# A residual added by accumulating transfers from memory instead of by VectorE

## Chip, core and metric

The kernel runs on one core of a Trainium2 chip. The metric is the device time of one execution in microseconds (us), the median of several runs. Five engines work side by side, each through its own queue in order: TensorE (PE; its weight loads are shown apart as PEld), VectorE (DVE), ScalarE (ACT), GpSimd (POOL) and SyncE (SP), which here only issues transfers. A tile in on-chip memory has 128 partitions; PSUM is the small memory that TensorE writes.

## What is computed

Multi-query attention with a residual, over 64 batches of 128 tokens with 512 features, 16 heads of width 64, one key and one value head shared by all of them:

```python
xn = layernorm(x, g_in)
q  = (xn @ Wq).reshape(b, n, H, DH).transpose(0, 2, 1, 3) * scale
kv = xn @ Wkv                      # k, v, each with one null row ahead
sim = einsum('bhid,bjd->bhij', q, k) + bias     # causal and key masks
out = einsum('bhij,bjd->bhid', softmax(sim), v) # -> (b, n, 1024)
return x + layernorm(out @ Wo, g_out)
```

All is float32. The change concerns the last line: `layernorm(out @ Wo, g_out)` of batch `b` is held in a tile `y_b` of 128 x 512, and `x[b]`, 256 KB in memory, is added to it before the store.

## The kernel before

The work goes in 32 steps of two batches each, called pairs; `body(d)` (L1311) is one step of a software pipeline, written out by hand, and `turn(d)` (L1024) is the short piece ahead of it. Every engine runs its instructions in the order in which these functions name them. In step `d` four pairs are under way: `a, b = 2d, 2d + 1` are in the scores and softmax, `p, p + 1 = 2d - 2, 2d - 1` in the output product, `l, l + 1 = 2d - 4, 2d - 3` in the output norm, the residual and the store, and batches of a coming group of four (`g`) have their input normed, transposed and projected. The residual is done in this way in steps 2 to 29, for 56 batches; the last two steps and the tail have code of their own, which the change leaves alone.

A step is even or odd (`h = d % 2`). They differ in two places that matter here:

- In an **odd** step up to 27, SP sends the normed and transposed tokens of the next group to memory and back: `tokens_out` (L333, tile `xd`, 1024 KB out) and `tokens_in` (L339, tile `xT`, four transfers of 256 KB in), where the latter wait for the former.
- In an **even** step, GpSimd has more to do: `token_sum` (L485), `token_sums_inner` (L556) and, from step 4 to 28, `token_sums_last` (L617), whose four subtractions write `xM` and `xS` for the matmuls `pm` of `last_product` (L633).

GpSimd also does `out_sum` (L904, four sums of tile `oT` for the output product), `scale` (L769, the softmax's factor onto the scores `s`) and `bias_add` (L676). VectorE's `blocks_T` (L783) transposes the scaled scores; behind it in VectorE's queue stands `out_keep("X", "yu2", ...)` (L945, L948), which copies the PSUM tile `pyX` to `kyu` before product 7 is added to `pyX`.

The output side of a pair: `out_product` (L918) makes seven products in PSUM tiles `pyX`, `pyY` and `pyw`; `out_part` (L952, the addition at L966) writes halves of `y_b`. For batch `p + 1` it reads `pyX` near the step's end, and the last product, number 4, may be added to `pyX` only after that. Tiles `y` come from a pool of three buffers, so `y` of `p + 1` gets the buffer of `y` of `l = p - 2`, and its first `out_part` waits until the store of `l` has read it. In the next step `pair_stats` and `pair_pow` make the norm's numbers, `pair_norm` (L990, ScalarE) writes the normed rows to a PSUM tile `yn`, `pair_gain` (L996) multiplies `yn` in place by the gain `gob`, `pair_residual` (L999) adds `res` and writes `y`, and `store` (L1002, on SP) sends it out. `load_res` (L126) loads `res` for the step after, at the end of SP's part of the step.

Of the kernel before, what the change touches and what calls it, by code (L numbers as in the profile page):

```python
# [11 lines left out]
ALU = mybir.AluOpType  # L12
# [5 lines left out]
def kernel(  # L18
# [59 lines left out]
    nc = tc.nc  # L78
# [34 lines left out]
    xs, res, m8s = {}, {}, {}  # L113
# [12 lines left out]
    def load_res(b):  # L126
        pool, tag = (rp, "res")
        if b >= B - 5:
            pool, tag = (gp, "xT") if b == B - 1 else (xp, "x")
        res[b] = pool.tile([P, DIM], FP, tag=tag, name=f"res_{b}")  # L130
        nc.sync.dma_start(out=res[b], in_=x[b])
# [20 lines left out]
    gob = const.tile([P, DIM], FP, name="gob")  # L152
# [186 lines left out]
    def tokens_in(g):  # L339
        xT[g] = gp.tile([P, GB, KC, N], FP, tag="xT", name=f"xT_{g}")  # L340
        xd = xds.pop(g).rearrange("(i p) j e -> j p i e", p=Q)
        for j in range(NQ):
            nc.sync.dma_start(
                out=xT[g][j * Q : (j + 1) * Q].rearrange("p i c n -> p i (c n)"),
                in_=xd[j],
            )
# [152 lines left out]
    def product(g, f, k, pool, tag, start=True):  # L499

        if start:
            prod[tag] = pool.tile([P, HT], FP, tag=tag, name=f"p{tag}_{g}_{f}_{k}")
        lo, hi = xT[g][:, 0 : GB // 2], xT[g][:, GB // 2 :]
        t1, t2, t3, t4 = (xS.get((g, i)) for i in range(1, 5))
        w, t = {
            1: (a11, lo[:, :, lo_k]),
            2: (a12, lo[:, :, hi_k]),
            3: (s4, hi[:, :, hi_k]),
            4: (a22, t4),
            5: (s1, t1),  # L510
            6: (s2, t2),
            7: (s3, t3),
        }[k]
        for kc in range(HK):
            nc.tensor.matmul(  # L515
                prod[tag],
                w[:, kc, f * P : (f + 1) * P],
                t[:, :, kc, :],
                start=(start and kc == 0),
                stop=(kc == HK - 1),  # L520
                skip_group_check=not start,
            )

    def keep(tag, name, slot=None):
        slot = slot or name
        kept[name] = bp.tile([P, HT], FP, tag=f"k{slot}", name=f"k{name}", bufs=1)
        nc.scalar.copy(kept[name], prod[tag])  # L527
# [251 lines left out]
    oT, ys = {}, {}  # L779
# [124 lines left out]
    def out_sum(p, k, eng=nc.gpsimd):  # L904

        h11, h12 = oT[p][:, 0], oT[p][:, 1]
        h21, h22 = oT[p + 1][:, 0], oT[p + 1][:, 1]
        if k == 0:
            yS[p] = bp.tile([P, HC, N], FP, tag="yS", name=f"yS_{p}", bufs=1)
        o, a, b, op = (  # L910
            (yS[p], h21, h22, ALU.add),
            (h11, yS[p], h11, ALU.subtract),
            (h21, h22, h11, ALU.subtract),
            (h12, h12, h11, ALU.subtract),
        )[k]
        eng.tensor_tensor(o, a, b, op)  # L916

    def out_product(p, k, pool, tag, start=True):  # L918
        key = "y" + tag
        if start and pool is ps_s:  # L920
            two = ps_s.tile([P, 2, DIM], FP, tag="s", name=f"py_{p}_{k}_s")
            prod[key] = two[:, 0, 0:HE]
        elif start:
            prod[key] = pool.tile([P, HE], FP, tag=tag, name=f"py{tag}_{p}_{k}")
        a, b = oT[p], oT[p + 1]
        h, w = {
            1: (a[:, 0], e11),
            2: (a[:, 1], e21),
            3: (a[:, 1], e22),
            4: (b[:, 1], sums_e[3]),  # L930
            5: (yS.get(p), sums_e[0]),
            6: (a[:, 0], sums_e[1]),
            7: (b[:, 0], sums_e[2]),
        }[k]
        for c in range(HC):
            nc.tensor.matmul(  # L936
                prod[key],
                h[:, c, :],
                w[:, c, :],
                start=(start and c == 0),  # L940
                stop=(c == HC - 1),
                skip_group_check=not start,
            )

    def out_keep(tag, name, slot):  # L945
        kept[name] = bp.tile([P, HE], FP, tag=f"k{slot}", name=f"k{name}", bufs=1)
        if name == "yu2":
            nc.vector.tensor_copy(kept[name], prod["y" + tag])  # L948
        else:
            nc.scalar.copy(kept[name], prod["y" + tag])  # L950
# [17 lines left out]
    yn = {}  # L968
# [25 lines left out]
        nc.scalar.activation(yn[b], ys[b], AF.Identity, bias=nmr, scale=rstd)  # L994

    def pair_gain(b):  # L996
        nc.vector.tensor_tensor(yn[b], yn[b], gob, ALU.mult)

    def pair_residual(b):  # L999
        nc.vector.tensor_tensor(ys[b], yn.pop(b), res.pop(b), ALU.add)  # L1000

    def store(b):  # L1002
        nc.sync.dma_start(out=out[b], in_=ys.pop(b))
# [17 lines left out]
    PAIRS = B // 2  # L1021
# [289 lines left out]
    def body(d):  # L1311

        a, b, p, l = 2 * d, 2 * d + 1, 2 * d - 2, 2 * d - 4
        g, h = d // 2 + 1, d % 2
        q, soft = g < NG, d > 0
        out, ln = 0 <= p <= P_LAST, 0 <= l <= P_LAST
# [48 lines left out]
            norm_nmr(m + 1)  # L1365
        if ln:
            pair_gain(l)
            pair_residual(l)
            store(l)
        if soft:  # L1370
            exps(b, 0, 0, 3)
        if out:
# [3 lines left out]
        if out:  # L1376
            out_product(p, 1, ps_y, "X")
            out_keep("X", "yp1", "yp1")
            out_sum(p, 1)
            out_sum(p, 2)  # L1380
        if q:
            product(g, f0, 6, ps_q, "a", start=False)
            keep("a", "u2")
# [14 lines left out]
        if ln:  # L1398
            pair_gain(l + 1)
# [16 lines left out]
            product(g, f1, 2, ps_w, "w")  # L1416
        if ln:
            pair_residual(l + 1)
            store(l + 1)
        if xw:  # L1420
            norm_apply(m + 1)
        if soft:
# [11 lines left out]
        if xw:  # L1434
            tokens_T(m + 1)
            if h == 1:
                tokens_out(g + 1)
                tokens_in(g + 1)
        if 0 <= p:
            for r in (p, p + 1):  # L1440
                load_res(r)
        nm = m + 2
# [236 lines left out]
    for d in range(1, PAIRS - 2):  # L1679
        turn(d)  # L1680
        body(d)
# [42 lines left out]
```

## Time and profile before

| | |
|---|---|
| runs | 1022.8, 1024.07 and 1023.01 us, median 1023.01 |
| profiled execution | span 1021.2 us; this span is the execution's own time, and the runs' median is 1.8 us above it |
| busy share of the span | PE 99%, PEld 88%, DVE 83%, POOL 75%, ACT 66% |
| granted TensorE clock | 0.999 of full speed |
| transfers | 100.86 MB, mean 99 GB/s, 98.47 MB of them on SP's queue; none issued by GpSimd |

The profile's page gives for each group of instructions its line, engine, operation, tiles, shape and count, then busy time, the mean duration and the idle time ahead of them with what ended it. The timeline lists instructions in order of time, with the idle time ahead in brackets. A step of two batches takes about 31.1 us.

### The profile page before, as it was taken

To read this page: it belongs to the slowest core of one execution; us is meant where nothing else is said; L and a number is where in the kernel's file an instruction comes from. 1 tells how busy PE (TensorE), PEld (TensorE's weight loads), DVE (VectorE), ACT (ScalarE), POOL (GpSimd) and SP (SyncE) were. 2 spreads that over 40 slices of the span, in tenths; PEclk is the share of its full clock that TensorE was granted. 3 is DMA by queue.
4 is the path that set the end of the run, shared out by engine and by line. 5 is a ranking of instruction groups with operands and counts; after the bars stand their busy time and mean duration, and the time that the engine had idled before them with its cause. 6 is when DMAs were issued, how large, how long until landed. Compare 5 with 4: busy or idle time off the path is not lost.

```text
span 1021.2 us, 31459 instructions
## 1 busy us (share of the span) xinstructions
PE 1012.8 (99%) x12333; PEld 899.6 (88%) x12333; DVE 845.8 (83%) x1958; ACT 673.1 (66%) x2753; POOL 769.2 (75%) x633
## 2 busy tenths in 40 slices
PE   9999999999999999999999999999999999999997
PEld 8888888888888888888888888888888888888886
DVE  6777888888888888888888888888898888977787
ACT  5766677656677665686656776566775657865583
POOL 4997768677686877859678696776868768686686
PEclk9999999999999999999999999999999999999999
DMA  7415143151531415225152341514315152140221
GB/s 219 139 30 151 67 122 112 36 154 63 144 98 69 123 56 152 88 74 140 36 152 85 109 120 32 164 63 138 102 50 134 64 152 89 71 111 24 69 85 62
DMA packets 73835, 100.86 MB, mean 99 GB/s; under 512 B 32212, under 2 KB 36056, under 8 KB 71896
## 3 DMA queue, kind: packets, MB, share of 16 engines
q1 hardware_dynamic: 73392, 98.47, 32.5%
q8 instruction: 96, 1.57, 0.6%
q14 instruction: 51, 0.42, 0.1%
q10 hardware_dynamic: 296, 0.40, 0.1%
HBM read 63.19 MB, written 33.55 MB: 95 GB/s over the span
## 4 chain that ended last, share of the span: by engine, by line
PE 96%; POOL 1%; DVE 1%; ACT 1%; issue 0%; DMA 0%; POOLq 0%; DVEq 0%; ACTq 0%
PE pyX L936 20%; PE pa L515 16%; PE pyY L936 10%; PE pc L515 10%; PE po L849 8%; PE pkv L363 6%; PE pyw L936 5%; PE pl L581 4%; PE pm L647 4%; PE ps L718 3%; PE pq L450 3%; PE sc_X L718 2%; PE sc_Y L718 2%; PE sc_a L718 1%; PE py_s L936 1%; ACT s L749 1%
## 5 line engine op out<-in xcount | busy, mean ns | idle before, releaser
L749 ACT ACTIVATE s<-s,nmax 128x65 f32<-128x65 f32 (+1 forms) x1024 | 372.2, 369 | 61.7 <-DVE nmax L740 61.7
L771 POOL TENSOR_TENSOR s<-s,rinv 128x512 f32<-128x512 f32 (+1 forms) x132 | 190.6, 1446 | 133.1 <-DVE rinv L767 133.1
L683 POOL TENSOR_TENSOR s<-biasp,mneg 128x1552 f32<-128x1552 f32 (+1 forms) x65 | 206.2, 3176 | 50.9 <-DVE s L733 26.9
L749 ACT ACTIVATION_READ_ACCUMULATOR s<-s,nmax 128x1 f32 x1024 | 197.1, 192 | 0.0
L787 DVE STREAM_TRANSPOSE sb<-s 128x1536 f32<-128x1536 f32 (+1 forms) x68 | 113.6, 1674 | 11.4 <-POOL s L771 11.4
L740 DVE TENSOR_REDUCE nmax<-s 128x8 f32<-128x1032 f32 (+1 forms) x128 | 121.8, 952 | 0.1
L964 ACT COPY y<-pyX 128x256 f32<-128x256 f32 x29 | 10.8, 372 | 167.5 <-PE pyX L936 129.7
L936 PE MATMUL pyX<-wT,oT 128*128 128x256 f32 x464 | 109.7, 379 | 0.0
L936 PE MATMUL pyX<-wo,oT 128*128 128x256 f32 x464 | 109.7, 379 | 0.0
L936 PEld LDWEIGHTS pyX<-wo,oT 128*128 128x128 f32 x464 | 86.0, 190 | 10.5
L936 PEld LDWEIGHTS pyX<-wT,oT 128*128 128x128 f32 x464 | 84.0, 190 | 9.2
L916 POOL TENSOR_TENSOR oT<-oT 128x512 f32<-128x512 f32 x64 | 80.6, 1277 | 3.9 <-PE pyw L936 1.6
L849 PE MATMUL po<-sb,vr 32*64 32x128 f32 (+1 forms) x3904 | 82.9, 308 | 0.2 <-DVE sb L787 0.2
L527 ACT COPY ku<-pa 128x256 f32<-128x256 f32 x118 | 43.4, 367 | 59.8 <-issue 30.8
L849 PEld LDWEIGHTS po<-sb,vr 32*64 32x64 f32 x3904 | 71.7, 130 | 9.4 <-issue 5.6
L536 DVE TENSOR_TENSOR qT<-pc,ku 128x256 f32<-128x256 f32 x118 | 48.2, 408 | 32.2 <-PE pc L515 19.7
L868 ACT ACTIVATE oT<-po,nv 128x512 f32<-128x512 f32 (+1 forms) x127 | 73.5, 655 | 0.4 <-PE po L849 0.2
L515 PE MATMUL pa<-xS,wq 128*128 128x256 f32 x264 | 67.8, 379 | 0.0
L597 DVE TENSOR_TENSOR qT<-pl,kp 128x128 f32<-128x128 f32 x112 | 32.1, 286 | 42.8 <-PE pl L581 41.9
L281 POOL TENSOR_TENSOR rstd<-rstd,nhalf 128x1 f32<-128x1 f32 x64 | 35.2, 557 | 42.0 <-DVE rstd L280 38.9
L363 PE MATMUL pkv<-xT,wkv 128*128 128x256 f32 x256 | 63.3, 391 | 0.0
L515 PE MATMUL pa<-xT,wq 128*128 128x256 f32 x236 | 60.6, 379 | 0.0
(207 smaller groups left out, 2588.9 us busy)
## 6 DMA issues: line engine op xcount, KB each, us to landing
res<-in_x_dram SPq DMA_DIRECT2D x64, 256.0 KB
out_dram<-y SPq DMA_DIRECT2D x63, 256.0 KB
x<-in_x_dram SPq DMA_DIRECT2D x62, 256.0 KB
xd<-xb SPq DMA_DIRECT2D x14, 1024.0 KB
xT<-xd SPq DMA_DIRECT2D x56, 256.0 KB
vr<-vd SPq DMA_DIRECT2D x64, 128.0 KB
kT<-kT SPq DMA_DIRECT2D x32, 64.0 KB
vd<-vb SPq DMA_DIRECT2D x32, 64.0 KB
```

The source lines that it names most:

```text
L363: nc.tensor.matmul(pkv, wkv[:, kc, :], xT[g][:, t : t + 2, kc, :], start=(kc == 0), stop=(kc == KC - 1),)
L515: nc.tensor.matmul(prod[tag], w[:, kc, f * P : (f + 1) * P], t[:, :, kc, :], start=(start and kc == 0), stop=(kc == HK - 1), skip_group_ch ...
L683: nc.gpsimd.tensor_tensor(S[b][:, :, keys], biasp[:, :, keys], mneg[:, t, keys] .unsqueeze(1) .broadcast_to([P, R8, keys.stop - keys.start ...
L718: nc.tensor.matmul(home[r][u * DH : (u + 1) * DH, f, :], qT[g, f, t // 2][rows, t % 2, hf, u], kT[rows, 0 : nk // Q, t, :], start=True, st ...
L740: nc.vector.tensor_reduce(nmax[b][:, hf], S[b][:, :, WITH_NULL[hf]], AX.X, ALU.max, negate=True)
L749: nc.scalar.activation(row, row, AF.Exp, bias=nmax[b][:, hf, k : k + 1], accum_out=rsum[b][:, hf, k : k + 1],)
L771: nc.gpsimd.tensor_tensor(sv, sv, rinvs[b, hf][:, lo:hi].unsqueeze(2).broadcast_to([P, hi - lo, sv.shape[2]]), ALU.mult,)
L787: nc.vector.transpose(sbs[b][:, :, lo:hi].rearrange("p j e q -> p e j q"), S[b][:, lo:hi, 1 : ROW - 1].rearrange("p e (j k) -> p e j k", k=Q),
L849: nc.tensor.matmul(po[s][rows, to : to + n], vr[g][quad, t, PLACE[j], :], sb[quad, slots, r * NF : (r + 1) * NF, :], start=(turn == 0), st ...
L868: nc.scalar.activation(to, src, AF.Identity, bias=nv2)
L916: eng.tensor_tensor(o, a, b, op)
L936: nc.tensor.matmul(prod[key], h[:, c, :], w[:, c, :], start=(start and c == 0), stop=(c == HC - 1), skip_group_check=not start,)
```

## The change

`pair_gain` now writes its product from `yn` to `y`. `pair_residual` becomes a transfer that GpSimd issues: it reads `x[b]` from memory and adds it onto `y_b` in place. Both stores move from their places behind the residuals to one place behind `tokens_out` and `tokens_in`. The loads of `res` in the steady steps go; step 29 still loads the two that the last steps use. The transfer of `l` is issued behind `out_sum(p, 2)` instead of the addition directly behind `pair_gain(l)`; that of `l + 1` keeps its place in the code.

```diff
     def pair_gain(b):
-        nc.vector.tensor_tensor(yn[b], yn[b], gob, ALU.mult)
+        nc.vector.tensor_tensor(ys[b], yn.pop(b), gob, ALU.mult)

     def pair_residual(b):
-        nc.vector.tensor_tensor(ys[b], yn.pop(b), res.pop(b), ALU.add)
+        nc.gpsimd.dma_start(out=ys[b], in_=x[b], accum_op=ALU.add)
...
         if ln:
             pair_gain(l)
-            pair_residual(l)
-            store(l)
...
             out_sum(p, 1)
             out_sum(p, 2)
+        if ln:
+            pair_residual(l)
...
         if ln:
             pair_residual(l + 1)
-            store(l + 1)
...
                 tokens_out(g + 1)
                 tokens_in(g + 1)
-        if 0 <= p:
+        if ln:
+            store(l)
+            store(l + 1)
+        if d == PAIRS - 3:
             for r in (p, p + 1):
                 load_res(r)
```

SP's queue in an odd step before the change; `y_3115` and `y_3237` are the two batches stored, `xd` and `xT` the tokens' way out and in, `vd` the values (the numbers are the program's and differ between the two programs):

```order
L396 DMA kT<-kT 64x4x64
L137 DMA m_5_3441<-in_mask_BxS_bk_dram 128x512
L1003 DMA out_dram<-y_3115 128x512
L1003 DMA out_dram<-y_3237 128x512
L335 DMA xd_3544<-xb_3140 128x2048
L343 DMA xT_3546<-xd_3544 32x4x512 x4
L131 DMA res_3551<-in_x_dram 128x512
L131 DMA res_3553<-in_x_dram 128x512
L122 DMA x_3555<-in_x_dram 128x1x512
L122 DMA x_3557<-in_x_dram 128x1x512
```

The same step of the changed kernel:

```order
L396 DMA kT<-kT 64x4x64
L137 DMA m_5_3417<-in_mask_BxS_bk_dram 128x512
L335 DMA xd_3518<-xb_3118 128x2048
L343 DMA xT_3520<-xd_3518 32x4x512 x4
L1003 DMA out_dram<-y_3094 128x512
L1003 DMA out_dram<-y_3213 128x512
L122 DMA x_3527<-in_x_dram 128x1x512
L122 DMA x_3529<-in_x_dram 128x1x512
```

The stores have gone from ahead of `xd` to behind `xT`, into the places of the two loads of `res`.

VectorE's queue near the end of that odd step in the changed kernel; in brackets stand the counters on which an instruction waits, DMAHW for transfers that SP issued, DMASW for those of GpSimd:

```order
L966 TENSOR_TENSOR y_3497<-pyY_5_3563,kyu_3596 128x256 [waits PE_49]
L972 BN_STATS sto_3616<-y_3497 128x6 [waits DVE_49]
L974 BN_AGGR mvo_3618<-sto_3616 128x2 [waits DVE_49]
L976 TENSOR_SCALAR rstdo_3620<-mvo_3618 128x1 [waits DVE_49]
L966 TENSOR_TENSOR y_3627<-pyX_1_3460,kyp_3568 128x256 [waits DMAHW7_49,DMASW2_49,PE_49]
L536 TENSOR_TENSOR qT_3_1_3394<-pc_3_5_3570,ku_3576 128x4x64 [waits PE_49]
L663 TENSOR_TENSOR qT_3_0_3393<-pm_1_3536,ku_3603 128x2x64 [waits PE_49]
L663 TENSOR_TENSOR qT_2_0_3391<-pm_1_3536,qT_2_0_3391 128x2x64
L787 STREAM_TRANSPOSE sb_3636<-s_3195 128x8x6x32 [waits Pool_49]
```

The order is as before. `y_3627` has the buffer of `y_3094`, so the second L966 waits for the store of `y_3094`, which before stood ahead of `xd` and now stands behind `xT`.

GpSimd's queue in an even step before, from the sums of the output product to the scaling of the scores' second half:

```order
L916 TENSOR_TENSOR oT_2160<-yS_2239,oT_2160 128x512
L916 TENSOR_TENSOR oT_2160<-oT_2160 128x512 x2
L771 TENSOR_TENSOR s_1963<-s_1963,rinv_0_2266 128x8x64
L627 TENSOR_TENSOR xM_2283<-xS_3_2241 128x128
L627 TENSOR_TENSOR xS_3_2241<-xS_3_2241 128x128
L627 TENSOR_TENSOR xM_2283<-xS_3_2241,xM_2283 128x128 x2
L771 TENSOR_TENSOR s_1733<-s_1733,rinv_1_2332 128x8x128
```

The same stretch in the changed kernel:

```order
L916 TENSOR_TENSOR oT_2148<-yS_2225,oT_2148 128x512
L916 TENSOR_TENSOR oT_2148<-oT_2148 128x512
L1000 DMA y_1847<-in_x_dram 128x512
L916 TENSOR_TENSOR oT_2148<-oT_2148 128x512
L771 TENSOR_TENSOR s_1951<-s_1951,rinv_0_2253 128x8x64
L627 TENSOR_TENSOR xM_2270<-xS_3_2227 128x128
L627 TENSOR_TENSOR xS_3_2227<-xS_3_2227 128x128
L627 TENSOR_TENSOR xM_2270<-xS_3_2227,xM_2270 128x128 x2
L1000 DMA y_1972<-in_x_dram 128x512
L771 TENSOR_TENSOR s_1725<-s_1725,rinv_1_2316 128x8x128
```

Two transfers stand in GpSimd's queue that were not there, the first ahead of the last sum, the second ahead of the scaling of `s`.

## The prediction

> **What bounds the kernel now.** I read the page first: its busy shares, and the chain of work that ended last.
>
> ```profile
> PE 1012.8 (99%) x12333; PEld 899.6 (88%) x12333; DVE 845.8 (83%) x1958; ACT 673.1 (66%) x2753; POOL 769.2 (75%) x633
> PE 96%; POOL 1%; DVE 1%; ACT 1%; issue 0%; DMA 0%; POOLq 0%; DVEq 0%; ACTq 0%
> ```
>
> TensorE works through, and the chain is 96% TensorE. Then the waits: who held up TensorE at all in the steady steps.
>
> ```profile
> PEld sc_Y L718 <- issue: 10.1, 32, 0.3
> PEld pkv L363 <- DVE s L733: 4.3, 25, 0.2
> ```
>
> The largest wait of TensorE for another engine is 4.3 us in all. That is the ceiling of what freeing VectorE can bring; the issue gaps are TensorE's own. So the question is not what the change saves, but whether it makes TensorE wait.
>
> **What is taken from VectorE.**
>
> ```profile
> L1000 DVE TENSOR_TENSOR y<-yn,res 128x512 f32<-128x512 f32 x56 | 38.5, 687 | 1.0
> ```
>
> 56 additions of 687 ns, 38.5 us of VectorE's time, two per step. `pair_gain` keeps its instruction. By the row above the 38.5 us lie beside TensorE; VectorE soon waits for TensorE again in each step. I count them at nothing. The bytes read for the residual stay the same, on another queue.
>
> **Odd steps: the store behind the tokens.** The timeline of SP's queue in one odd step, and the wait ahead of `xT` over all 14 groups:
>
> ```profile
> 573.31 2.66 SPq L1003 DMA_DIRECT2D out_dram<-y  x2
> 577.44 0.33 SPq L335 DMA_DIRECT2D xd<-xb  x1
> 581.35 1.75 SPq L343 DMA_DIRECT2D xT<-xd  x4
> 583.14 0.90 SPq L131 DMA_DIRECT2D res<-in_x_dram  x2
> ...
> L343 SPq EVENT_SEMAPHORE  x14: 17/3505/4683, 80.3 to 888.6; - x14
> ```
>
> SP stands some 3.5 us (median) until `xd` has landed, then issues four `xT`. The store of `l` went out at 573.3; now it takes the place of the first `res`, at 583.14, behind 4 x 256 KB in the same queue. What waits for it is the `out_part` of `p + 1`, which reuses its buffer (the rows from VectorE's and TensorE's timelines):
>
> ```profile
> 587.06 0.42 DVE L966 TENSOR_TENSOR y<-pyX,kyp 128x256 f32<-128x256 f32 x1 [0.17 <-PE pyX L936]
> ...
> 588.77 1.77 DVE L787 STREAM_TRANSPOSE sb<-s 128x1536 f32<-128x1536 f32 x1
> ...
> 588.16 1.89 PE L936 MATMUL pyX<-wT,oT 128*128 128x256 f32 x8
> ```
>
> L966 ran at 587.06 and TensorE's product 4 at 588.16 must follow it, since it adds onto the `pyX` that L966 reads. When does the transfer in the place of the first `res` land? From the busy time by stretches (last two numbers: share of the transfer engines, GB/s):
>
> ```profile
> 582.00:583.00 1.00, 1.00 (x7) 0.87 (x6) 1.00 (x3) 0.25 (x2) 0.00 (x0) 1.00 0.42 82
> 583.00:584.00 1.00, 1.00 (x7) 0.92 (x6) 0.35 (x3) 0.37 (x1) 0.74 (x1) 1.00 0.77 256
> 584.00:585.00 1.00, 1.00 (x6) 0.87 (x6) 0.75 (x3) 0.00 (x0) 1.00 (x1) 1.00 1.04 213
> 585.00:586.00 1.00, 1.00 (x7) 0.87 (x6) 0.64 (x2) 0.00 (x0) 1.00 (x2) 1.00 1.06 219
> 586.00:587.00 1.00, 1.00 (x6) 0.90 (x5) 0.82 (x3) 0.00 (x0) 1.00 (x1) 1.00 1.06 213
> 587.00:588.00 1.00, 1.00 (x8) 0.90 (x7) 0.50 (x2) 0.00 (x0) 1.00 (x1) 1.00 1.06 211
> 588.00:589.00 1.00, 1.00 (x7) 0.92 (x7) 0.98 (x4) 0.00 (x0) 0.83 (x2) 1.00 1.00 317
> 590.00:591.00 1.00, 1.00 (x69) 1.00 (x72) 0.79 (x2) 0.37 (x1) 0.38 (x1) 1.00 0.47 116
> ```
>
> Up to 588 they add up to 1194 KB. Four `xT` and one more transfer are 5 x 262 = 1311 KB, reached at 588.4 at the earliest; the queue empties in the stretch from 590. I take 589.3 for the landing, between the two, because the slowest of 16 engines decides and later transfers share the last stretch. L966 then ends at 589.7, and with 0.1 for the signal TensorE starts product 4 at 589.8 instead of 588.16: 1.65 us lost. It is lost for good, since TensorE has no idle time to give it back; behind L966 on VectorE stand two small additions and L787, which keep their distance to TensorE.
>
> To this comes the accumulating transfer of `l + 1`. GpSimd will issue it right when `xd` is on its way out (below), and another 262 KB then share the engines. `xd` moves at 1049 KB in some 3.5 us, 300 KB per us, so this costs 0.9 us if each byte is moved once, nothing if it fits into gaps, and 1.8 us if the old value is read and the sum written back as two movements. I take 0.9, since the share of the engines leaves few gaps. **Per odd step 2.55 us**, from 1.0 (landing at 588.7, no slowing) to 4.1 (landing at 590.0, and 1.8).
>
> An odd step counts if it stores and has tokens: steps 3 to 27, so 13. **13 x 2.55 = 33 us** (13 to 53).
>
> **Even steps: GpSimd's issue time.** The timeline of GpSimd in one, and what follows on VectorE and TensorE:
>
> ```profile
> 543.50 2.51 POOL L916 TENSOR_TENSOR oT<-oT 128x512 f32<-128x512 f32 x2
> 545.97 1.04 POOL L771 TENSOR_TENSOR s<-s,rinv 128x512 f32<-128x512 f32 x1
> 546.97 0.45 POOL L627 TENSOR_TENSOR xM<-xS 128x128 f32<-128x128 f32 x1
> ...
> 548.87 1.91 POOL L771 TENSOR_TENSOR s<-s,rinv 128x1024 f32<-128x1024 f32 x1
> 553.08 1.90 POOL L771 TENSOR_TENSOR s<-s,rinv 128x1024 f32<-128x1024 f32 x1 [2.31 <-DVE rinv L767]
> ...
> 550.80 1.78 DVE L787 STREAM_TRANSPOSE sb<-s 128x1536 f32<-128x1536 f32 x1 [0.80 <-POOL s L771]
> 552.51 0.38 DVE L948 COPY kyu<-pyX 128x256 f32<-128x256 f32 x1
> ...
> 554.05 1.89 PE L936 MATMUL pyX<-wo,oT 128*128 128x256 f32 x8
> ...
> DVE sb L787 <- POOL s L771: 11.4, 13, 1.3
> ```
>
> GpSimd has no gap from 543.5 to 550.8. Both issues (first behind 544.75, the second ahead of 548.87) push the scaling at 548.87 by 2T, T being the time that one issue holds GpSimd. VectorE's L787 waited for that scaling already, in 13 steps, so L787 and the copy L948 behind it come 2T later. The copy ends at 552.89, and product 7 at 554.05 needs it: 1.1 us of slack. The loss is 2T - 1.1. The matmuls `pm` at 549.06, which need `xM`, meet one T and have 0.6 us; the later wait covers theirs. Ahead of the next scaling, at 553.08, GpSimd idled 2.31 us, so the delay is spent within the step.
>
> T is not in this trace. Its nearest rows are SP's issue, GpSimd's smallest instruction, one over 128 rows, and its longest:
>
> ```profile
> L131 SPq DMA_DIRECT2D res<-in_x_dram x64: 351/430/1275, 85.6 to 989.4; - x64
> L980 POOL TENSOR_TENSOR rstdo<-rstdo,nhalf 128x1 f32<-128x1 f32 x57 | 31.3, 548 | 0.0
> L916 POOL TENSOR_TENSOR oT<-oT 128x512 f32<-128x512 f32 x64 | 80.6, 1277 | 3.9 <-PE pyw L936 1.6
> L683 POOL TENSOR_TENSOR s<-biasp,mneg 128x1552 f32<-128x1552 f32 x63 | 202.9, 3222 | 49.0 <-DVE s L733 26.9 <-DVE sb L787 13.2 <-DMA vd<-vb 8.9
> ```
>
> Between 0.43 and 3.2 us I take T = 1.2, nearest to 1.277: the issue handles 128 rows in software. **13 x (2.4 - 1.1) = 17 us**; at T = 0.43 nothing, at 3.2 it is 69. The Trainium skill, "DMA: Bandwidth & Descriptors", section "Latency and other measured facts", gives some 1 us to the first byte for transfers that GpSimd issues. No run here shows it; with T = 1.0 the term would be 12 us.
>
> In odd steps GpSimd has room for 2T (2.69 us idle in the second row):
>
> ```profile
> 574.88 1.05 POOL L771 TENSOR_TENSOR s<-s,rinv 128x512 f32<-128x512 f32 x1
> 578.62 1.90 POOL L771 TENSOR_TENSOR s<-s,rinv 128x1024 f32<-128x1024 f32 x1 [2.69 <-DVE rinv L767]
> ```
>
> With one T ahead of 574.88, that scaling ends at 577.1 and the transfer of `l + 1` is issued by 578.3, beside `xd`. In even steps the store is in time: the first issue ends by 546; give its landing and that of the store each the 3.5 us that `xd` needs for four times the bytes, and `y` is free at 553, against L966 at about 556, as far behind TensorE's product 7 as in the odd step. The loads of `x` behind it are needed most of a step later.
>
> **Sum.** 33 + 17 = 50 us on a span of 1021.2, and 1.8 from the span to the median of the runs: **about 1073 us**, 5% slower.
>
> **Rivals.**
>
> *Not slower.* In odd steps the decisive point is 587.06: if the store does not queue up behind `xT` but lands as fast as `xd` with four times the bytes, 3.5 us after its issue, at 586.6, nothing waits for it. With T up to 0.55 the even steps are free too, and the time is 1023, at best 1019 by the 4.3 us of TensorE's waits. Against it: from 584 to 589 the engines are at a share of 1.0, so no transfer passes another there. 8%, 3 of them for faster.
>
> *Only the store.* T under 0.55 and the wait in odd steps as computed: 1023 + 33 = 1056. For it: SP's issues take 0.43. Against it: GpSimd does not finish even a 128x1 instruction in less than 0.55. 17%.
>
> *A dear issue.* With T = 2.2, even steps lose 3.3 each, 43 us, odd ones as before: 1099. An accumulation may need twice the work per row of a plain load. 17%.
>
> *The clock falls.* At the end of the trace, TensorE's last matmuls and the clock behind them (the number ahead of the share):
>
> ```profile
> 1013.71 1.99 PE L936 MATMUL pyc<-wT,oT 128*128 128x256 f32 x8 [0.57 <-DVE y L966]
> ...
> 1018.00:1019.00 1.00, 0.00 (x0) 0.00 (x0) 0.45 (x2) 0.00 (x0) 0.00 (x0) 0.73 0.05 19
> 1019.00:1020.00 1.00, 0.00 (x0) 0.00 (x0) 0.00 (x0) 0.00 (x0) 0.00 (x0) 0.50 0.71 243
> ```
>
> The last matmul ends at 1015.70, and a mean of 0.73 from 1018 says that the clock halved near 1018.5, after 2.8 us. A stall of 2.55 stays just short of it. If it reaches it in every odd step, and the half clock lasts as long again, each loses 1.4 more: 18 us, 1091. The Trainium skill, "TensorE: Matmul & The Clock Gate", Part 1, puts the idle time at about 3.4 us; by that the stalls stay free of it, and the trace's 2.8 is the shorter. 8%.
>
> **How the numbers follow.** The forecast has 50%, "only the store" 17, "a dear issue" 17, "the clock falls" 8, "not slower" 8. The range from 1040 (low ends of the store's wait, T at 0.6) to 1122 (53 us and T = 2.3) holds all but "not slower" and the far ends. About 0.2% is what a measurement of this kernel tells from no change. Faster 3%, same 5%, slower 92%.
>
> **What would show it.** In the changed kernel's profile: TensorE waiting for VectorE's L966 at `pyX` in 13 odd steps, 2 to 3 us each, with VectorE itself waiting there for the transfer of `y`; TensorE waiting for the copy L948 in 13 even steps, about 1.3 us; VectorE's wait for GpSimd at L787 grown from 0.9 to 2T more; steps without tokens (29) at their old length. Wrong would be: no wait at `pyX`, or a long wait in SP for the accumulating transfer itself, or waits of GpSimd at its own transfers.

## The result, and the profile after

The changed kernel takes **1094.18 us** (median of four runs, 1093.61 to 1096.56), against 1022.9 us for the kernel before on the same chip: a ratio of 1.070, with a 95% interval of 1.068 to 1.071. It is 7% slower. The forecast was 1073, its range 1040 to 1122. The profiled execution's span is 1091.8 us, 70.6 more than before; the forecast had 50.

The page's busy shares and its chain of work that ended last:

```profile
PE 1036.0 (95%) x12333; PEld 909.9 (83%) x12333; DVE 812.2 (74%) x1902; ACT 673.4 (62%) x2753; POOL 820.1 (75%) x689
PE 53%; POOL 18%; DMA 15%; DVE 9%; SPq 2%; issue 2%; ACT 1%; POOLq 0%; DVEq 0%; ACTq 0%
```

VectorE has lost 33.6 us of work, and GpSimd has gained 50.9. The chain was 96% TensorE; now 42% of it runs through GpSimd, transfers and VectorE. TensorE is also busy 23 us longer with the same 12333 matmuls, and that needs an explanation of its own (mostly the clock, below). The waits (us in total, times, longest), those of this case picked out:

```profile
DVE y L966 <- DMA out_dram<-y: 55.1, 13, 4.8
PEld pyX L936 <- DVE y L966: 45.6, 13, 4.0
PE pyX L936 <- DVE y L966: 42.9, 13, 3.8
DVE sb L787 <- POOL s L771: 30.7, 15, 2.4
...
PEld pyX L936 <- DVE kyu L948: 7.3, 12, 0.7
```

The first three rows are one stall seen three times: the store keeps the buffer, VectorE's L966 waits for it, and TensorE's product 4 waits for L966, in 13 steps, 3.5 us each (45.6 / 13). The last two are the even steps' delay behind GpSimd, a small matter.

**An odd step.** SP's queue, TensorE's and VectorE's rows around the stall, and SP's wait ahead of `xT` over all steps (min, median, max in ns):

```profile
546.32 0.33 SPq L335 DMA_DIRECT2D xd<-xb  x1
552.12 1.75 SPq L343 DMA_DIRECT2D xT<-xd  x4
553.97 0.85 SPq L1003 DMA_DIRECT2D out_dram<-y  x2
...
560.45 0.42 DVE L966 TENSOR_TENSOR y<-pyX,kyp 128x256 f32<-128x256 f32 x1 [4.68 <-DMA out_dram<-y]
...
560.93 3.68 PE L936 MATMUL pyX<-wT,oT 128*128 128x256 f32 x8 [3.72 <-DVE y L966]
...
L343 SPq EVENT_SEMAPHORE  x14: 17/5267/5399, 80.4 to 952.4; - x14
```

The stores leave at 553.97, behind `xT`, and L966 runs 6.5 us later. The wait for `xd` was 3505 ns before; it is 5267 now, 1.76 us more. And product 4 is slow once it starts: its eight matmuls take 3.68 us, where they took 1.89. The stretches behind the stall show why (the third number from the end is the granted clock; the first busy share is TensorE's):

```profile
557.00:558.00 1.00, 0.21 (x2) 0.02 (x1) 0.00 (x0) 0.00 (x0) 0.74 (x2) 1.00 1.03 207
558.00:559.00 1.00, 0.00 (x0) 0.00 (x0) 0.00 (x0) 0.00 (x0) 0.00 (x0) 1.00 1.01 291
559.00:560.00 1.00, 0.00 (x0) 0.00 (x0) 0.00 (x0) 0.00 (x0) 0.00 (x0) 1.00 0.97 329
560.00:561.00 1.00, 0.07 (x1) 0.07 (x1) 0.55 (x2) 0.00 (x0) 0.00 (x0) 0.99 0.78 188
561.00:562.00 1.00, 1.00 (x3) 0.82 (x4) 1.00 (x4) 0.00 (x0) 0.00 (x0) 0.50 0.27 99
...
564.00:565.00 1.00, 1.00 (x31) 0.46 (x32) 0.00 (x0) 0.35 (x1) 1.00 (x1) 0.80 0.26 89
```

In the two microseconds in which TensorE idles throughout, the transfer engines are full (shares of 1.01 and 0.97): the transfers are the bound. When TensorE resumes, its clock is halved for some 3.4 us. The record of the clock has ten such stretches among the 13 steps, and the mean clock is 0.982, where it was 0.999.

**An even step.** GpSimd's rows, then VectorE's and TensorE's behind it:

```profile
511.48 1.27 POOL L916 TENSOR_TENSOR oT<-oT 128x512 f32<-128x512 f32 x1
512.69 0.89 POOL L1000 DMA_DIRECT2D y<-in_x_dram  x1
513.33 1.57 POOL L916 TENSOR_TENSOR oT<-oT 128x512 f32<-128x512 f32 x1
...
517.83 0.89 POOL L1000 DMA_DIRECT2D y<-in_x_dram  x1
518.45 2.21 POOL L771 TENSOR_TENSOR s<-s,rinv 128x1024 f32<-128x1024 f32 x1
...
520.69 1.78 DVE L787 STREAM_TRANSPOSE sb<-s 128x1536 f32<-128x1536 f32 x1 [2.33 <-POOL s L771]
522.39 0.39 DVE L948 COPY kyu<-pyX 128x256 f32<-128x256 f32 x1
...
522.83 1.99 PE L936 MATMUL pyX<-wo,oT 128*128 128x256 f32 x8 [0.26 <-DVE kyu L948]
```

From the third sum's start to the end of the scaling GpSimd takes 9.18 us (511.48 to 520.66); before, the same stretch took 7.28 (543.50 to 550.78). The difference of 1.90 is two issues, so T = 0.95: 0.89 in its own row, the rest in the instruction behind it (1.57 for a sum of 1.27).

**Where the 70.6 us are.** I measured each step on TensorE's timeline from its first `pkv` (the keys' and values' projection) to the next one's. The 13 odd steps are 62.6 us longer in all. Of these the waits above are 45.6, which leaves 17 us for the ten halved stretches, 1.7 each; 3.413 us at half speed hold back just that. The single steps agree: in three of them the clock was not halved, and they are 3.35 us longer on average, with waits of 3.31; the other ten are 5.25 longer, with waits of 3.57. Twelve even steps went from 31.08 to 31.61 on average, 6 us. The rest, 1.8, lies at the end (from the first `pkv` of step 29 on 85.8 us, before 84.0).

### The profile page after: what moved, and what is told of

Its sections match the earlier page's. It is cut to its first block, busy times and chain, and to the rows that moved or that the text cites. A ratio compares the mean times of both kernels' runs of the same rounds, so it can differ in the third digit from the quotient of the medians.

```text
span 1091.8 us, 31429 instructions
## 1 busy us (share of the span) xinstructions
PE 1036.0 (95%) x12333; PEld 909.9 (83%) x12333; DVE 812.2 (74%) x1902; ACT 673.4 (62%) x2753; POOL 820.1 (75%) x689
## 3 DMA queue, kind: packets, MB, share of 16 engines
q0 software_dynamic: 8064, 14.68, 9.1%
q8 instruction: 96, 1.57, 0.6%
## 4 chain that ended last, share of the span: by engine, by line
PE 53%; POOL 18%; DMA 15%; DVE 9%; SPq 2%; issue 2%; ACT 1%; POOLq 0%; DVEq 0%; ACTq 0%
PE pyX L936 13%; PE pa L515 8%; DMA xd<-xb 7%; DMA out_dram<-y 7%; PE po L849 5%; PE pc L515 5%; POOL s L771 4%; PE pkv L363 4%; POOL oT L916 4%; PE pyw L936 3%; PE pq L450 3%; POOL xS L497 2%; DVE sb L787 2%; PE pyY L936 2%; DVE s L733 2%; SPq L343 2%
## 5 line engine op out<-in xcount | busy, mean ns | idle before, releaser
L771 POOL TENSOR_TENSOR s<-s,rinv 128x512 f32<-128x512 f32 (+1 forms) x132 | 202.0, 1532 | 119.6 <-DVE rinv L767 119.6
L936 PE MATMUL pyX<-wT,oT 128*128 128x256 f32 x464 | 124.2, 416 | 42.9 <-DVE y L966 42.9
L936 PEld LDWEIGHTS pyX<-wT,oT 128*128 128x128 f32 x464 | 91.2, 206 | 57.6 <-DVE y L966 45.6
L916 POOL TENSOR_TENSOR oT<-oT 128x512 f32<-128x512 f32 x64 | 89.3, 1396 | 3.1 <-PE pyw L936 0.8
```

The lines of the kernel that those rows point to most:

```text
L771: nc.gpsimd.tensor_tensor(sv, sv, rinvs[b, hf][:, lo:hi].unsqueeze(2).broadcast_to([P, hi - lo, sv.shape[2]]), ALU.mult,)
L936: nc.tensor.matmul(prod[key], h[:, c, :], w[:, c, :], start=(start and c == 0), stop=(c == HC - 1), skip_group_check=not start,)
```

## The experiments

My theory after the result had three parts: the stores behind `xT` and the slower `xd` make the odd steps' stall (46 us), the issues on GpSimd the even steps' loss, and the stall itself halves the clock. The rivals: that the stall is the whole loss, that the clock matters little, or that it is the accumulation as such, not the place of the stores.

### A buffer of its own for the second half

```diff
+            elif b % 2 and b < B - 7:
+                ys[b] = rp.tile([P, DIM], FP, tag="res", name=f"y_{b}")
```

The odd batches' `y` take the buffers that `res` no longer needs, so that L966 does not wait for the store.

> The changed kernel, but y of the odd batches takes its buffers from the two that held res, so that no y waits for a store of its own step. Theory (TensorE waits because the store of l stands behind the tokens in SP's queue and y of p + 1 needs l's buffer; the halved clock follows from that wait): the waits at pyX for L966 go, the clock stays at full speed, and what is left is GpSimd's issue time in the even steps, 12 x 0.6 us: 1028 to 1032 us. Rival (GpSimd's issues are the larger part of the loss): above 1060.

Measured: 1037.4 us, ratio 1.014 (1.012 to 1.015), span 1035.1. Neither VectorE nor TensorE stalls there any more; what is left of this case is GpSimd's part:

```profile
DVE sb L787 <- POOL s L771: 30.4, 15, 2.6
...
PEld pyX L936 <- DVE kyu L948: 7.0, 11, 0.9
```

The clock is back at 0.998 although `xd` still waits as long as in the change. So the buffer's wait, and what comes with it, is 57 of the 70.6 us. It came out 5 us above what I expected: the even steps are 8.5 us longer than before, up to 1.1 each (in the change, 6), the odd ones 3.5 and the end 1.8.

### The stores moved, nothing else

The kernel before, with both stores behind the tokens and ahead of `load_res`; VectorE still adds the residual.

```diff
         if ln:
             pair_gain(l)
             pair_residual(l)
-            store(l)
...
             pair_residual(l + 1)
-            store(l + 1)
...
                 tokens_in(g + 1)
+        if ln:
+            store(l)
+            store(l + 1)
         if 0 <= p:
```

> The kernel before, with its loads of res and VectorE's additions, but both stores behind the tokens as in the change (ahead of the loads of res). Theory (a wait of 1.65 us per odd step from the store's place alone, and the accumulating transfer beside xd adds the rest): 13 x 1.65 = 21 us, 1044 (1038 to 1050), xd landing in some 3.5 us as before, no half clock. Rival (the store's place alone makes the whole wait of 3.5 us and the half clock): 1085 to 1090.

Measured: 1048.36 us, ratio 1.024 (1.022 to 1.026), near the top of the range that I expected. Its waits, SP's wait ahead of `xT`, and one stretch of time:

```profile
DVE y L966 <- DMA out_dram<-y: 32.3, 13, 2.9
...
PEld pyX L936 <- DVE y L966: 22.8, 13, 2.1
...
L343 SPq EVENT_SEMAPHORE  x14: 17/3484/3948, 81.1 to 914.8; - x14
...
540.00:541.00 1.00, 1.00 (x4) 0.81 (x3) 1.00 (x2) 0.00 (x0) 0.00 (x0) 0.50 0.69 168
```

The move alone, with no accumulating transfer in the program, makes the stall: 1.75 us in each of 13 steps. `xd` has its old 3.5 us. The even steps keep their length. And even here the clock was halved twice, which I had not expected (the last row stands behind one such stall), though no wait at `pyX` is longer than 2.1.

### One store ahead of the tokens

The change, with only the store of `l` moved ahead of `tokens_T(m + 1)` and `tokens_out`.

```diff
         if xw:
             tokens_T(m)
+        if ln:
+            store(l)
         if xw:
             tokens_T(m + 1)
...
         if ln:
-            store(l)
             store(l + 1)
```

> The changed kernel, but the store of l stands ahead of the tokens' way out in SP's queue; that of l + 1 stays behind their way in. Theory (the place in the queue makes the wait): as with buffers of its own, 1028 to 1034; SP may hold the tokens back a little while it waits for the accumulation of l. Rival (an accumulated y lands so late that its store is late in any place): above 1050.

Measured: 1037.73 us, ratio 1.014 (1.013 to 1.016), the same as with the buffers of its own, and like it some 4 us above what I expected. So of the two moved stores that of `l`, whose buffer is reused in the same step, makes the stall; that of `l + 1` may stay behind the tokens.

### Plain loads by GpSimd

The second experiment, with the loads of `res` issued by GpSimd at the places of the accumulating transfers. Same bytes, same queue, nearly the same times of issue, but nothing is added on the way; VectorE adds.

```diff
-    def load_res(b):
+    def load_res(b, queue=nc.sync):
...
-        nc.sync.dma_start(out=res[b], in_=x[b])
+        queue.dma_start(out=res[b], in_=x[b])
...
             out_sum(p, 2)
+            load_res(p, nc.gpsimd)
...
             pair_residual(l + 1)
+        if out:
+            load_res(p + 1, nc.gpsimd)
```

> The kernel with only the stores moved, where GpSimd issues the loads of res for the next step, plain, at the places at which the change issues its accumulating transfers. Theory (an accumulating transfer takes the transfer engines twice as long as a plain one, since the old value is read too): xd lands in 4.3 to 4.5 us, between 3.5 and 5.3, GpSimd's queue has half the share of the engines that it has in the change (4.5 instead of 9.1%), TensorE waits some 2.6 us per odd step, 1070 to 1080. Rival (any transfer from GpSimd's queue slows xd so much): xd 5.3 us, 1090 to 1095.

Measured: 1068.57 us, ratio 1.045 (1.043 to 1.046), just below the range that I expected. GpSimd's queue on the page (packets, MB, share of 16 engines' span), landing, SP's wait, TensorE's, and how long an issue holds GpSimd (min, median, max in ns):

```profile
q0 software_dynamic: 4640, 15.21, 5.6%
...
res<-in_x_dram POOLq DMA_DIRECT2D x58, 256.0 KB, 3.3
...
L343 SPq EVENT_SEMAPHORE  x14: 17/4340/4462, 80.3 to 929.2; - x14
...
PEld pyX L936 <- DVE y L966: 34.3, 13, 3.1
...
L131 POOL DMA_DIRECT2D res<-in_x_dram x58: 577/596/742, 76.6 to 991.9; - x58
```

and the same of the change:

```profile
q0 software_dynamic: 8064, 14.68, 9.1%
...
y<-in_x_dram POOLq DMA_DIRECT2D x56, 256.0 KB, 4.2
```

A plain transfer of 256 KB takes the 16 engines 1066.5 x 5.6% / 58 = 1.03 us, an accumulating one 1091.8 x 9.1% / 56 = 1.77. Beside a plain one `xd` is 0.84 us later than before, beside an accumulating one 1.76. So the slowing of `xd` follows the engine time that the other transfer takes (0.84 beside 1.03, 1.76 beside 1.77), and the accumulation takes 1.7 times that of a load. Its issue costs more too: a plain one holds GpSimd 0.60 us, an accumulating one 0.89.

### The second transfer issued earlier

The change, but in odd steps the transfer of `l + 1` is issued 2 us earlier, so that more of it is over when `xd` goes out.

```diff
         if ln:
             pair_gain(l + 1)
+        if ln and h == 1:
+            pair_residual(l + 1)
...
-        if ln:
+        if ln and h == 0:
             pair_residual(l + 1)
```

> The change, but in odd steps the accumulating transfer of l + 1 is issued right behind its gain, some 2 us earlier, ahead of the fourth sum of the output product, so that most of it has landed when the tokens' xd goes out. Theory (the transfer of l + 1 moves beside xd and that is what makes xd 1.76 us later): SP's wait ahead of xT falls from a median of 5267 to some 4200 (3500 to 4600), the store and with it TensorE's wait at pyX by as much, from 3.4 to about 2.4 per odd step, 13 us in all, and fewer stalls halve the clock: some 1073 us (1066 to 1082). Rival (xd is late for another reason, or the bytes wait for each other wherever the transfer stands): the wait ahead of xT stays at 5.2 and the time at 1094.

Measured: 1080.85 us, ratio 1.055 (1.054 to 1.057); the profiled execution, 1084.26 us with a span of 1082.0, is the longest of the four.

```profile
L343 SPq EVENT_SEMAPHORE  x14: 17/4512/4788, 80.3 to 943.1; - x14
...
PEld pyX L936 <- DVE y L966: 38.1, 13, 3.5
```

`xd` gained 0.75 us, TensorE's stall 0.58. The direction and most of the size hold; the clock recovered little (0.985 against 0.982; up to 0.991 in the other runs). Set side by side, SP's median wait for `xd` and TensorE's stall per odd step rise together:

| kernel | `xd`, us | stall, us |
|---|---|---|
| stores moved only | 3.48 | 1.75 |
| plain loads by GpSimd | 4.34 | 2.64 |
| second transfer earlier | 4.51 | 2.93 |
| the change | 5.27 | 3.51 |

### The stall filled with matmuls

The change, with 24 matmuls ahead of product 4 in the odd steps from 5 on. They multiply the gain tile with itself into a PSUM tile that nothing reads, so they add work and no result; they only keep TensorE busy.

```diff
+    def fill(n):
+        for _ in range(n):
+            nc.tensor.matmul(
+                prod["a"][:, 0:P], gob[:, 0:P], gob[:, 0:P], start=True, stop=True
+            )
...
+        if deeper and h == 1 and xw:
+            fill(24)
```

> The changed kernel with 24 matmuls of 128x128 into a dead PSUM tile in 12 of the 13 odd steps, ahead of product 4, where TensorE waits for L966; some 2.6 us of work within a wait of 3.4. Theory (idle TensorE halves its own clock, and each of the nine halved stretches costs some 1.7 us): at most one halved stretch is left, 1094 - 15 = 1079 (1077 to 1082). Rival (the halved stretches cost nothing that counts, or come from something else): 1094, with the halved stretches still there.

Measured: 1103.04 us, ratio 1.078 (1.076 to 1.079), slower than the change. Why, is in the groups and waits:

```profile
L971 PE MATMUL pa<-gob 128*128 128x128 f32 x576 | 66.3, 275 | 0.0
...
PEld pyX L936 <- DVE y L966: 3.7, 1, 3.7
```

Each matmul of mine is two instructions, and a step's worth kept TensorE 66.3 / 12 = 5.5 us, longer than the stall it should fill. The halved stretches are gone from the filled steps (mean clock 0.997), but the run says nothing on the price of the clock.

### The stall half filled

The same with 12 matmuls.

> As the kernel with the filled stall, with 12 matmuls instead of 24: each took 0.22 us there, so 24 made 5.3 us and outlasted the wait; 12 make 2.65 us and end within it. Theory (idle TensorE halves its own clock): the steps stay as long as the store makes them, the half-clock stretches go in the 12 filled steps, 1094 - 15 = 1079 (1077 to 1083). Rival (the halved stretches cost nothing that counts): 1094.

Measured: 1088.1 us, ratio 1.064 (1.062 to 1.066), 6 us faster than the change with 288 more matmul instructions on TensorE.

```profile
L971 PE MATMUL pa<-gob 128*128 128x128 f32 x288 | 34.1, 275 | 0.0
...
PEld pyX L936 <- DVE y L966: 16.5, 13, 3.4
```

The fill takes 2.8 us per step, and in the 12 filled steps 1.1 us of the stall stay open (13.1 / 12), too little to halve the clock (0.999). So the halved clock costs time: take it away and the kernel is faster, with more work. But 6 us is not the 17 that the lengths of the steps gave, nor the 15 that I expected. By those lengths the odd steps became 9 us shorter in all and the even ones 2 us longer. The odd ones are still 4.1 over those of before, where the change's own steps at full clock were 3.35 over: the fill adds some 0.8 itself, of which VectorE's longer wait for the store (58.1 against 55.1 us in all) shows 0.2. The even ones lose more, I suppose, because GpSimd no longer gains a lead while TensorE runs at half clock; that is argued, not shown. So this run sets the price of the clock at 6 us or more, and the lengths of the change's own steps set it at 17.

### Each transfer in two halves

The first experiment (own buffers), with each accumulation cut into two column halves: twice the issues, half the bytes in each.

```diff
-        nc.gpsimd.dma_start(out=ys[b], in_=x[b], accum_op=ALU.add)
+        for half in (lo_e, hi_e):
+            nc.gpsimd.dma_start(
+                out=ys[b][:, half], in_=x[b][:, half], accum_op=ALU.add
+            )
```

> The kernel with y's own buffers, each accumulating transfer cut into two of 128 x 256, so four issues per step. Theory (an issue costs GpSimd by rows or by transfer, not by bytes): each of the four takes some 0.9 us again, an even step loses 4 x 0.93 - 1.1 = 2.6 instead of 0.8 to 1.0, 1037 + 13 x 1.7 = 1059, and odd steps begin to lose as well, since 3.7 us exceed GpSimd's 2.7 us of idle time. Rival (by bytes): 0.45 each, 1037.

Measured: 1062.88 us, ratio 1.039 (1.037 to 1.040). The issues, of the halves and of the change's whole transfers, and two waits of this experiment:

```profile
L1003 POOL DMA_DIRECT2D y<-in_x_dram x112: 868/1171/1867, 108.6 to 984.7; - x112
...
PEld pyX L936 <- DVE kyu L948: 20.7, 13, 1.9
...
PEld pm L647 <- POOL xM L627: 13.7, 13, 1.3
```

```profile
L1000 POOL DMA_DIRECT2D y<-in_x_dram x56: 855/891/1205, 108.5 to 1017.4; - x56
```

Half the bytes hold GpSimd no shorter (1.17 us against 0.89). The price goes by transfer, or by its 128 rows, not by byte. I expected 1059 by that and 1037 by the bytes. The even steps are 33.6 us longer than in the kernel before, 2.6 each as expected; the odd ones, for which I expected a loss too, 0.8 in all.

### The issues out of the way

The first experiment, and in even steps both transfers and both stores behind `scale(a, 1)`, at the point where GpSimd idles 2.3 us.

```diff
+        if ln and h == 0:
+            pair_residual(l)
+            pair_residual(l + 1)
+            store(l)
+            store(l + 1)
```

(and `if ln` becomes `if ln and h == 1` at their old places).

> The kernel with y's own buffers, and in the even steps both accumulating transfers issued behind the scaling of a's second half, where GpSimd idles 2.3 us, with their stores behind the loads of x. Theory (what is left at 1037 is GpSimd's issue time, two of 0.93 us in its chain without a gap): 1023 to 1025, no wait of TensorE for the copy L948, VectorE's wait for GpSimd at the transpose back at 0.9 us; at best 1019 if TensorE's 4 us of waits for VectorE go too. Rival (the accumulating transfers disturb by their traffic): 1033 to 1037.

Measured: 1028.32 us, ratio 1.005 (1.004 to 1.006), span 1025.2; I expected 1023 to 1025. The last row is GpSimd's `DRAIN` at the program's end (min, median, max of three, in ns; the longest counts), and below it stands that of the kernel before:

```profile
DVE sb L787 <- POOL s L771: 9.1, 12, 1.3
...
PEld po L849 <- issue: 7.0, 35, 0.9
...
L1729 POOLq DRAIN  x3: 40/102/5421, 1019.0 to 1024.9; - x3
```

```profile
L1719 POOLq DRAIN  x3: 34/78/824, 1016.8 to 1020.8; - x3
```

VectorE's wait for GpSimd is below the 11.4 us of the kernel before, the even steps have their old 31.08, and no wait for the copy L948 is left. So the issues in GpSimd's way were the even steps' whole loss (the stores, moved alone, had cost them nothing). Still 4 us are missing to the kernel before. Of these 1.8 lie behind the last matmul, as in the change: GpSimd's closing `DRAIN` takes 5.42 us, where it took 0.82, and ends 1.8 us behind those of the other engines. It is 0.82 with only the stores moved, 5.42 in every program with 56 accumulating transfers, 5.58 with the 58 plain ones and 7.83 with the 112 halves: it goes with the transfers that GpSimd issues. The other 2.1 are 0.2 to 0.8 in each of five odd steps. TensorE pauses at `po`, the products with the values, for nothing that the trace shows (7.0 us in all, longest 0.9, against 5.6 and 0.3 before); I did not find the cause. Rid of both losses, the kernel is at best where it was: the 33.6 us taken from VectorE buy nothing, and no version here beats the kernel before.

## Why the prediction was right in sign and low in size

- **VectorE's 38.5 us bring nothing: right.** The last experiment is that case by itself.
- **Odd steps, the place of the store: right.** Forecast 1.65 us for each of 13 steps; the stores moved alone gave 1.75.
- **Odd steps, the slowing of `xd`: this is the step that failed.** The forecast took 0.9 us, "if each byte is moved once", and named 1.8 "if the old value is read and the sum written back as two movements". The trace has 1.76 and a transfer that takes 1.77 us of the engines, where a plain load takes 1.03 and would have slowed `xd` by 0.84. My 0.9 was the price of a plain load, and the change does not issue one. With it the waits of the odd steps came out at 45.6 us instead of 33.
- **Even steps: right place, too dear.** T was taken as 1.2 and is 0.95, and the loss by the prediction's own 2T - 1.1 would be 0.8 per step. With the stall gone it was 8.5 us in all, within the change 6 in twelve steps, not 17 in 13. The Trainium skill, "DMA: Bandwidth & Descriptors", section "Latency and other measured facts", has some 1 us to the first byte for transfers that GpSimd issues; by the sum made with it (12 us) I would have been nearer. It is not the same quantity, though: what counts here is how long GpSimd is held, and the rows above show that.
- **"The clock falls" came true, beside the forecast, not in its place.** I gave it 8%, because the end of the trace before has 2.8 us of idling ahead of a falling clock. That was the time of one case, no threshold: waits of 3.2 to 4.0 us halved the clock in ten steps of 13, and waits of 2.1 did so in two of the steps with the stores moved alone. The Trainium skill, "TensorE: Matmul & The Clock Gate", Part 1, counts idleness in free-running windows of about 3.4 us. The halved stretches are that long, 3.413 us, but by a rule of a whole idle window the stall of 2.1 could not have halved the clock; the measurement decides, and the last section has what it shows. I left the clock's share (17 us by the steps) out of the sum; as an addition to the forecast it should have stood in the range of the main case.
- **The rivals.** "Not slower" fell by the 13 waits, "only the store" by the even steps' loss, "a dear issue" by T = 0.95.
- **The sum**: 33 + 17 = 50 forecast; 46 + 6 + 17 and 1.8 at the end make up the 70.6 measured, to within rounding. The time was missed by 13 us in the odd steps' wait, 17 by the clock and 1.8 at the end, and the even steps were priced 11 too high. That the total came as near as it did is in part luck: the 11 too many made up for a third of the 32 that were missing. The range's low end, by its own terms 13 us and 1, should have read 1037 instead of 1040; nothing hangs on it.

## What to carry to other kernels

Before you move an issue to another place in a queue, follow the buffer, not the data: here nobody needed the stored rows, but the next writer needed their buffer, and a buffer of its own, or one store left ahead of the tokens, brought back 57 of the 70.6 us. Work taken from an engine that nobody waits for is worth nothing, while the same work on a transfer queue or an engine that stands in the chain is paid for in full: price an accumulating transfer as more than a load, in engine time and in its issue. And a stall of TensorE of two microseconds or more can cost beyond its length, since its clock may be halved behind it.

## What the runs showed of the hardware that I had not expected

- An accumulating transfer of 256 KB takes the 16 engines 1.77 us against 1.03 for a plain one, lands 4.2 us after its issue against 3.3, and is cut into 144 packets (8064 / 56) against 80 (4640 / 58).
- Its issue holds GpSimd no shorter when the 128 rows are 1 KB long (1.17 us median) than when they are 2 KB long (0.89), and the instruction behind it took 0.3 longer in the even step shown (1.57 for 1.27). A plain issue of 2 KB rows holds it 0.60.
- With transfers by GpSimd in the program, GpSimd's closing `DRAIN` takes 5.42 us (56 of them) to 7.83 (112) instead of 0.82.
- The clock was halved for some 3.4 us behind stalls as short as 2.1 us (2 of 13 steps), and not behind three of the change's, in steps 3.2 to 3.5 us longer than before.
- What these traces set apart is not the length of a stall but how much of it falls into one division of a fixed grid. The halved stretches of a trace start whole multiples of 3.413 us apart (in the change 20, 59, 79, 99 and so on behind the first). Cut along its own grid, each trace gives TensorE's busy time and clock by divisions; three rows are of the change, the last two of the stores moved alone:

```profile
557.57:560.98 3.41, 0.05 (x1) 1.00 0.95 263
560.98:564.39 3.41, 3.41 (x8) 0.50 0.29 104
...
356.18:359.59 3.41, 1.54 (x7) 1.00 0.72 223
...
536.23:539.64 3.41, 1.51 (x10) 1.00 1.01 335
539.64:543.05 3.41, 3.41 (x8) 0.50 0.47 137
```

  From TensorE's first step to its last matmul, the eleven traces hold 26 halved stretches. TensorE was idle for at least 1.90 us of the division ahead of each of them; of all other divisions, some 3300, one had 1.97 us of idleness and the rest at most 1.87. So a stall of 3.2 us that a border splits in two (the third row, 1.87 idle) leaves the clock alone, and one of 1.9 within a division (the fourth) halves it.
